# A four-layer graph network: step 1 of layer 3 propagates through half-size products, with sums of adj kept in DRAM

## The chip, the cores and the metric

The kernel runs on one core of a Trainium2 chip. A core has five engines that each take their own instructions in order: TensorE (PE, with its weight loads shown apart as PEld), VectorE (DVE), ScalarE (ACT), GpSimd (POOL) and SyncE (SP), which here only issues transfers. They wait for each other through semaphores. The metric is the device time of one execution in microseconds (us).

## The reference

The input is a node matrix x (3327 x 256) and one dense matrix adj (3327 x 3327) that all four layers share. Each layer normalises its input, takes the positive part and adds what the layer makes of it:

```python
h = relu(layernorm(x)); x = x + layer0(h, adj)     # adj @ (h W0' + b)
h = relu(layernorm(x)); x = x + layer1(h, adj)     # tanh(adj*adj), filtered, @ (tanh(h Wp + b) Wg), relu
h = relu(layernorm(x)); x = x + layer2(h, adj)     # D^-1/2 (adj+I) D^-1/2 @ (h W2'), relu
h = relu(layernorm(x)); x = x + layer3(h, adj)
# layer 3, on X = h:
R = adj + eye;  R = R / R.sum(-1, keepdims=True)
Xf = Xa = X;  Z = 0
for n in range(2):
    A  = top_p_attention(Xa)     # softmax((Xa W1'W2')(Xa W3')'), largest entries until 0.9, renormalised
    Xf = R @ Xf
    Xa = A @ Xa
    Z  = Z + Xf @ U1[n].T + Xa @ U2[n].T
out = layernorm(X + Z) * ln_g + ln_b
```

## The kernel before

The 3327 nodes are padded to T = 26 tiles of P = 128; H = 13 is half of them. adj comes transposed and cut into blocks: `adj_t[m, :, k, :]` is the block that carries tile k into tile m, and the diagonal of adj is full. All arithmetic is in fp32, and each fp32 product of two blocks shows in the profile as two matmul instructions.

**Layers 0 to 2** (`products`, L555) take row tiles in pairs, p and p + 13. A pair's four quadrants of adj (a11, a12, a22, a21, each 13 blocks) times the 2 x 2 quadrants of the right side (13 tiles deep, halves of 128 columns wide) are formed with 7 products in place of 8 (`Product`, L502): three of the left operands are quadrants (a11, a12, a22) and four are sums (s1 = a21 + a22, a21' = a11 − a21, s2 = s1 − a11, s4 = a12 − s2); the sums on the right are made once per layer. `Feed` (L451) loads the quadrants in three cuts of 5, 4 and 4 blocks through the SP queue, up to two cuts ahead (`load`), and VectorE makes the sums one cut ahead (`add`, L485–488). These matmuls are 128 columns wide (L520).

**Layer 3** (`layer_3_in`, L841) has two steps. Each has 26 rows of tiles, and for each row:

- attention: logits of one row tile (L914), their exponentials on ScalarE (L935), a search for the smallest kept entry (`search_steps`), a pass that zeroes the others (L1013), then the row turned block by block (L178, copied by ScalarE at L181) and multiplied with the node values (L189; `Rows.begin` and `Rows.finish`);
- propagation: R times the node tiles (`propagated_steps`, L1058): 26 matmuls of 128 x 128 by 128 x 256, with adj's row tile loaded as two slabs of 13 blocks (832 KB) from a pool of three buffers; GpSimd adds the identity to the diagonal block (L1068).

In step 1 the propagated tile is scaled by the inverse row sum on ScalarE (`xf`, L1110), turned (L138) and multiplied with U1 (`sums`, L1122), which writes `fs`, the operand of step 2's propagation. `AttentionOfFirstStep` scales attention's result by 1/den (`xa`, L1080), turns it, makes the keys of step 2 (`node`) and, with U2, `vs` and `z` (L1099, L1100; z goes to DRAM).

The search of one row starts with the row's sum (`total`, L952), a mean and a spread of the logits from it, and the first bound t: Ln, Ln and Exp on ScalarE (L953–955), `t = 2 mean − c` on VectorE (L956), Exp on ScalarE (L957). Two passes of ScalarE over the row follow (L968, L973), then VectorE's: one pass with the next bound (L984), extraction of candidates in four parts (L993, L997), five rounds of eight largest (L1002, L1005), and L1013.

**Order.** In layer 3 the instructions of TensorE stand in the order of the program (`manual_schedule` with PE alone); the hooks in `plan` (a dictionary from the number of a matmul to functions) interleave the rest with the matmuls of a row. The other engines' order is chosen by a planner, pushed by `high_priority` and `issue_after`. The first EARLY = 4 propagated tiles come ahead of the first attention row; LATE = 4 come at the end of step 1. Attention runs AHEAD = 3 rows ahead of its use. The rows in APART = (3, 7, 11, 15, 19) carry no propagation: they start the next logits and go on to the next row. Between the steps stands a branch on flags (L1254) behind which lies a fallback for searches that failed (`if_failed`).

Of the kernel before, what the change touches and what calls it, by code (L numbers as in the profile page):

```python
# [45 lines left out]
def kernel(  # L46
# [54 lines left out]
    hT_dram = dram.tile([P, T, NC, P], F32, name="hT_dram")  # L101

# [162 lines left out]
    def layers_0_to_2(again):  # L265
# [120 lines left out]
        class Pair:  # L386


            def __init__(self, layer, p, rhs, x2):
                self.layer, self.p, self.rhs = layer, p, rhs  # L390
                self.pool = work, "xT", 2
                self.name = f"{tag}{layer}_{p}"
                if layer == 3:
                    self.xn = pair_of(rhs.rows, p)
                    normed(self.name, x2, self.xn)
                    nc.vector.tensor_scalar(self.xn, self.xn, 0.0, None, ALU.max)
# [46 lines left out]
            def keys(self):  # L443
                for i in range(2):
                    m = self.p + i * H
                    add_nodes(kT0, ksum0, self.xT[:, :, i * P : (i + 1) * P], m, f"{self.name}_{i}", bank)
# [4 lines left out]
        class Feed:  # L451
# [3 lines left out]
            def __init__(self, layer, order, load_x, change=None, count=None):  # L455
                self.layer, self.order, self.load_x = layer, order, load_x
                self.change, self.count = change, count
                self.quads, self.ready, self.x2, self.done = {}, {}, {}, [0, 0]
# [17 lines left out]
            def add(self, p, c):  # L476
# [11 lines left out]
                nc.vector.tensor_tensor(s4, a12, s2, ALU.subtract)  # L488
                self.ready[p, c] = a11, a12, s4, a22, s1, s2, a21
# [115 lines left out]

        IN_ORDER = [(p, c) for p in range(H) for c in range(len(CUTS))]
# [56 lines left out]
        if not again:  # L663
# [31 lines left out]
            feed = Feed(0, order + IN_ORDER[2 * len(CUTS) :], load_x, count=count0)  # L695
# [67 lines left out]
        else:  # L763
# [57 lines left out]
            2, P, rhs2, Feed(2, IN_ORDER, from_rows(x2_dram), count=count2), finish2(rhs2), left,  # L821
# [19 lines left out]
    def layer_3_in(tag, big, ep, w3, sm3, h3, kT0, ksum0, left, at_end):  # L841


        fs = new_nodes(f"fs{tag}")[:, :, :D]
# [21 lines left out]
        gs = big.tile([P, D], F32, name="gs")  # L866
        nc.scalar.dma_start(gs, ln_g.partition_broadcast(P))
        bs = big.tile([P, D], F32, name="bs")
        nc.scalar.dma_start(bs, ln_b.partition_broadcast(P))
# [69 lines left out]
        def search_steps(step, m, e, parts, st, dens, alone):  # L939
# [12 lines left out]
            nc.vector.tensor_reduce(total, parts, AX.X, ALU.add)  # L952
# [3 lines left out]
            nc.vector.scalar_tensor_tensor(t, mean, 2.0, c, ALU.mult, ALU.subtract)  # L956
            nc.scalar.activation(t, t, AF.Exp)  # L957
# [70 lines left out]
        def failed(step, st):  # L1028
# [14 lines left out]
            pf = ps_acc.tile([P, 512], F32, tag="acc", name=f"pf_{step}")  # L1043
# [14 lines left out]
        def propagated_steps(acc, step, m, xf):  # L1058
# [3 lines left out]
            for n, k in enumerate(order):  # L1062
# [7 lines left out]
                yield n  # L1070

# [31 lines left out]
        class PropagationOfFirstStep:  # L1103


            def __init__(self, m, acc):
                self.m = m
                self.xf = w3.tile([P, D], F32, tag="xf", name=f"xf_{m}")
                with tc.high_priority():
                    nc.scalar.activation(self.xf, acc[:, :D], AF.Copy, scale=rinv[:, m : m + 1])  # L1110
                self.hT = w3.tile([P, NC, P], F32, tag="hT", name=f"hT_{m}")
                nc.sync.dma_start(self.hT, hT_dram[:, m])

# [4 lines left out]
            def sums(self):  # L1118
                acc = one_bank(f"u1_{self.m}")
                parts = [(xT[:, c, :], u1s[:, s, c, :]) for s, xT in enumerate((self.hT, self.xT)) for c in range(NC)]  # L1120
                for i, (xT, u) in enumerate(parts):
                    nc.tensor.matmul(acc[:, :D], xT, u, start=(i == 0), stop=(i == len(parts) - 1))  # L1122
                with tc.high_priority():
                    nc.scalar.copy(fs[:, self.m, :], acc[:, :D])

        def finish3(m, y, acc, name):
# [4 lines left out]
            x3 = w3.tile([P, D], F32, tag="xf", name=f"x3_{name}")  # L1131
# [49 lines left out]

        def keep_of_equal(e, t, target, s, name):
# [3 lines left out]
            rank, eq = (  # L1186
                slabs.tile([P, H, P], F32, tag="slab", name=f"{k}_{name}").rearrange("p k m -> p (k m)")
                for k in ("rank", "eq")
            )
            rank, eq = rank.bitcast(I16), eq.bitcast(U8)[:, :NP]  # L1190
# [88 lines left out]
        with tc.manual_schedule(engines=PE_ALONE):  # L1279
# [23 lines left out]
            def passes_apart(step, finder, late=False):  # L1303

# [5 lines left out]
                def more_of_first():  # L1310
                    with tc.high_priority(), tc.issue_after(last_turned[-1].ins):
                        next(finder)
# [257 lines left out]
```

## Time and profile before

| what | value |
|---|---|
| median of three runs | 2642.61 us (2639.8 to 2642.98) |
| the profiled execution | 2643.87 us |
| its span in the profile | 2641.7 us |
| PE busy | 2564.9 us (97%) |
| DVE busy | 2035.0 us (77%) |
| ACT busy | 1034.2 us (39%) |
| POOL busy | 284.2 us (11%) |
| step 1 of layer 3, from the first attention row (1028.4 to 1834.5 us) | 806.1 us |
| moved by DMA | 273.43 MB, mean 104 GB/s |

The span runs from the first to the last instruction in the profile; the execution has some 2 us around it. A row of the groups reads: line, engine, operation, output from inputs, shape, count, then busy us in all and mean ns of one, then the idle time before it and what ended most of it. In the waits view a row names the engine and line that waited, what for, the us in all, how many times, and the longest. In the timeline a row has its start, its length, engine, line, operation and count, and in brackets the idle time before it. DMA shares are of the core's 16 DMA engines.

### The profile page before, as it was taken

The page shows a single profiled execution, that of the slowest core. Times are in us where ns is not written, and L with a number is a line of the kernel's source. Part 1 is how long each engine was busy: PE and PEld are TensorE (multiplying, and loading weights), DVE is VectorE, ACT ScalarE, POOL GpSimd, SP SyncE. Part 2 cuts the span into 40 slices and gives each one's busy share as a digit, 9 for nine tenths or more (in the row PEclk, how much of TensorE's full clock was granted, in tenths as well). Part 3 has the DMA queues.
Part 4 walks back from the last instruction along what each step waited for, and adds up shares of the span by engine and source line. Part 5 has one row for each costly group of instructions (what it writes and reads, how often), then busy time and mean ns, then how long its engine had stood idle before and what let it go on. Part 6 is the DMA issues. An engine that isn't in the chain of part 4 may idle for free. (4 is left out here: it accounts for less than half of the span.)

```text
span 2641.7 us, 42749 instructions
## 1 busy us (share of the span) xinstructions
PE 2564.9 (97%) x15979; PEld 2213.1 (84%) x15979; DVE 2035.0 (77%) x5495; ACT 1034.2 (39%) x1873; POOL 284.2 (11%) x435
## 2 busy tenths in 40 slices
PE   6999999999999999999999999999999999999997
PEld 6999999999999987777777777787787888888786
DVE  6667689888877848787878778783888888888883
ACT  2110124343011115555555555553545454545541
POOL 2000010000000000000000000000032222223221
PEclk9999999999999999999999999999999999999999
DMA  6455546555566632111111111111221122122211
GB/s 221 139 165 168 155 146 191 168 163 175 178 198 197 198 110 85 61 36 61 59 61 35 60 36 61 34 61 66 79 75 66 64 90 70 64 70 84 70 65 52
DMA packets 141358, 273.43 MB, mean 104 GB/s; under 512 B 15427, under 2 KB 67904, under 8 KB 141120
## 3 DMA queue, kind: packets, MB, share of 16 engines
q1 hardware_dynamic: 115648, 252.49, 30.2%
q10 hardware_dynamic: 25472, 17.92, 2.2%
q8 instruction: 131, 2.15, 0.3%
q14 instruction: 107, 0.88, 0.1%
HBM read 248.20 MB, written 20.45 MB: 102 GB/s over the span
## 5 line engine op out<-in xcount | busy, mean ns | idle before, releaser
L181 ACT COPY eT_a<-pt_a 128x512 f32<-128x512 f32 (+1 forms) x364 | 196.1, 554 | 340.4 <-PE pt_a L178 340.2
L1069 PE MATMUL f<-h3a,slab3a 128*128 128x256 f32 x1352 | 324.3, 383 | 4.9 <-ACTq L1254 4.8
L189 PE MATMUL a<-h3a,eT_a 128*128 128x256 f32 x1352 | 321.5, 379 | 0.7 <-ACT eT_a L181 0.7
L189 PE MATMUL a<-vs,eT_a 128*128 128x256 f32 x1352 | 320.2, 381 | 0.2 <-ACT eT_a L181 0.2
L1069 PE MATMUL f<-fsa,slab3a 128*128 128x256 f32 x1352 | 312.7, 382 | 0.0
L1069 PEld LDWEIGHTS f<-h3a,slab3a 128*128 128x128 f32 x1352 | 246.6, 189 | 65.7 <-issue 28.9
L1069 PEld LDWEIGHTS f<-fsa,slab3a 128*128 128x128 f32 x1352 | 249.8, 189 | 52.7 <-issue 17.4
L997 DVE MAX8 cand_a<-w 128x8 f32<-128x128 f32 x1352 | 284.6, 279 | 3.9
L189 PEld LDWEIGHTS a<-h3a,eT_a 128*128 128x128 f32 x1352 | 245.7, 189 | 36.5 <-issue 6.7
L189 PEld LDWEIGHTS a<-vs,eT_a 128*128 128x128 f32 x1352 | 246.4, 190 | 31.7 <-ACT eT_a L181 0.7
L520 PE MATMUL acc_a<-tsa,s_a 128*128 128x128 f32 (+1 forms) x2028 | 268.5, 275 | 0.7 <-DVE tsa L332 0.7
L520 PE MATMUL acc_a<-tsa,a_a 128*128 128x128 f32 x2028 | 251.0, 275 | 2.0 <-DVE tsa L335 2.0
L520 PE MATMUL acc_a<-rhs,a_a 128*128 128x128 f32 (+1 forms) x2028 | 250.4, 276 | 0.0
L520 PEld LDWEIGHTS acc_a<-tsa,s_a 128*128 128x128 f32 x2028 | 247.4, 192 | 1.4 <-DVE tsa L332 1.1
L520 PEld LDWEIGHTS acc_a<-tsa,a_a 128*128 128x128 f32 x2028 | 239.6, 192 | 3.5 <-DVE tsa L335 2.6
L520 PEld LDWEIGHTS acc_a<-rhs,a_a 128*128 128x128 f32 x2028 | 238.4, 192 | 1.9 <-ACT rhs L412 0.4
L993 DVE SCALAR_TENSOR_TENSOR w<-e_a,t_a 128x896 f32<-128x896 f32 x208 | 224.8, 1081 | 3.9
L935 ACT ACTIVATE e_a<-pl_a 128x1024 f32<-128x1024 f32 x208 | 177.8, 860 | 113.5 <-PE pl_a L914 112.4
L178 PE MATMUL pt_a<-ident,e_a 128*128 128x128 f32 x1352 | 199.6, 273 | 1.9
L178 PEld LDWEIGHTS pt_a<-ident,e_a 128*128 128x128 f32 x1352 | 165.2, 141 | 39.5 <-ACT eT_a L181 9.5
L984 DVE SCALAR_TENSOR_TENSOR w<-e_a,t_a 128x3328 uint8<-128x3328 f32 x52 | 191.6, 3685 | 3.6
L1013 DVE SCALAR_TENSOR_TENSOR e_a<-e_a,all_least 128x3328 f32<-128x3328 f32 x52 | 191.6, 3685 | 1.9
(208 smaller groups left out, 3366.1 us busy)
## 6 DMA issues: line engine op xcount, KB each, us to landing
slab3a<-in_adj_t_dram SPq DMA_DIRECT2D x104, 832.0 KB, 6.0
a_a<-in_adj_t_dram SPq DMA_DIRECT2D x312, 256.0 KB, 3.4
a_a<-in_adj_t_dram SPq DMA_DIRECT2D x156, 320.0 KB, 3.4
x_dram<-x_a ACTq DMA_DIRECT2D x39, 256.0 KB, 3.2
x_a<-x_dram SPq DMA_DIRECT2D x26, 256.0 KB, 3.2
hT_dram<-xT_a ACTq DMA_DIRECT2D x26, 128.0 KB, 3.5
hT<-hT_dram SPq DMA_DIRECT2D x26, 128.0 KB, 2.0
z_dram<-z SPq DMA_DIRECT2D x26, 128.0 KB, 1.7
```

Of the source, the lines that this page charges most:

```text
L178: nc.tensor.transpose(pt[:, j, :], e[:, k * P : (k + 1) * P], ident)
L181: last_turned.append(nc.scalar.copy(eT[:, : len(blocks), :], pt[:, : len(blocks), :]))
L189: nc.tensor.matmul(acc[:, :width], ready[g][:, j, :], rhs[:, k, :], start=(k == 0), stop=(k == T - 1))
L520: nc.tensor.matmul(self.acc[:, g, at : at + wide], quads[n][:, k - CUTS[c][0], :], t, start=(k == 0 and n in (1, 4)), stop=(k == H - 1 and ...
L935: last_exp.append(nc.scalar.activation(dst, src, AF.Exp, accum_out=parts[:, c : c + 1]))
L984: nc.vector.scalar_tensor_tensor(junk, e, t, e, ALU.is_lt, ALU.mult, accum_out=got)
L993: nc.vector.scalar_tensor_tensor(w[:, : (b - a) * P], eg, t, eg, ALU.is_lt, ALU.mult, accum_out=below[:, g : g + 1])
L997: nc.vector.max(cand[:, 8 * k : 8 * k + 8], w[:, (k - a) * P : (k - a + 1) * P])
L1013: nc.vector.scalar_tensor_tensor(e, e, least, e, ALU.is_ge, ALU.mult, accum_out=st["kept"][:, m : m + 1])
L1069: nc.tensor.matmul(acc[:, :D], slab[g][:, j, :], xf[:, k, :], start=(n == 0), stop=(n == T - 1))
```

## The change

1. In step 1 of layer 3 the propagation of a pair of row tiles is made with 7 half-size products (`FirstStepsPair`), 13 blocks deep and 128 columns wide, in two phases: products 1, 2, 5, 4 (52 matmuls), then 7, 3, 6 (39); for the first pair 1, 2, 3, then 5, 4, 7, 6. A phase stands where one row tile's 26 matmuls stood. Each product has one slab of 13 blocks. ScalarE copies the first accumulator (`half`), VectorE forms the four results with five instructions (`whole`), and `scale` multiplies with the inverse row sums on ScalarE.
2. The sums on the right, of h3's halves, are made at the start of layer 3 (`combine_h3`) and take the buffer that held `fs`. `sums` now writes its result to DRAM through SP (rows 12 and 25 of `fs` directly), and `fs` is loaded into h3's buffer on ScalarE's queue at the start of step 2.
3. The sums on the left come from DRAM: layer 0 writes them for pairs 2, 4, ..., 12 and layer 2 for pairs 0, 1, 3, ..., 11 (`KEPT`), four transfers for each cut of a kept pair, on SP's queue (`Feed.add`).
4. In the search ScalarE makes `total` (with an accumulating copy) and t (with −c as the bias of an Exp); VectorE has no part in them.
5. The row after an APART row no longer has its passes later than other rows (`late`). One propagated tile moves from the next-to-last row to the one before it. In rows, the turn of a propagated tile comes two groups later, with its scaling ahead of it. gs and bs take the place of u1s and are loaded in step 2. The fallback's spare tiles come from elsewhere.

```diff
@@ Feed.add @@
                 nc.vector.tensor_tensor(s4, a12, s2, ALU.subtract)
+                if p in self.keep:
+                    for n, s in enumerate((s1, s2, a21, s4)):
+                        nc.sync.dma_start(s_dram[:, p, n, a:b, :], s)
                 self.ready[p, c] = a11, a12, s4, a22, s1, s2, a21
@@ products @@
+        KEPT = range(2, H, 2), [0, *range(1, H, 2)]
@@ layer_3_in @@
-            fs = new_nodes(f"fs{tag}")[:, :, :D]
+        ts = new_nodes(f"ts3{tag}").rearrange("p t d -> p (t d)")[:, : 4 * H * P]
+        ts = ts.rearrange("p (n k f) -> p n k f", n=4, k=H)
...
@@ search_steps @@
-            nc.vector.tensor_reduce(total, parts, AX.X, ALU.add)
+            nc.scalar.activation(parts, parts, AF.Copy, accum_out=total)
             nc.scalar.activation(mean, total, AF.Ln, scale=1.0 / N)
             nc.scalar.activation(lnv, mean, AF.Ln, bias=tiny, scale=2.0)
             nc.scalar.activation(c, lnv, AF.Exp, bias=ln_z, scale=0.5)
-            nc.vector.scalar_tensor_tensor(t, mean, 2.0, c, ALU.mult, ALU.subtract)
-            nc.scalar.activation(t, t, AF.Exp)
+            nc.scalar.activation(lnv, c, AF.Copy, scale=-1.0)
+            nc.scalar.activation(t, mean, AF.Exp, bias=lnv, scale=2.0)
@@ new in layer_3_in @@
+        PHASES = (1, 2, 5, 4), (7, 3, 6)
+        FIRST_PHASES = (1, 2, 3), (5, 4, 7, 6)
+        PLACE3 = {2: (0, 0), 1: (0, 1), 4: (0, 2), 5: (0, 3), 6: (1, 0), 7: (1, 1), 3: (1, 2)}
+
+        def combine_h3(a, b):
+            def part(i, j):
+                return h3[:, i * H + a : i * H + b, j * P : (j + 1) * P]
+
+            t1, t2, t3, t4 = (ts[:, n, a:b, :] for n in range(4))
+            nc.vector.tensor_tensor(t1, part(0, 1), part(0, 0), ALU.subtract)
+            nc.vector.tensor_tensor(t2, part(1, 1), t1, ALU.subtract)
+            nc.vector.tensor_tensor(t4, part(1, 0), t2, ALU.subtract)
+            nc.vector.tensor_tensor(t3, part(1, 1), part(0, 1), ALU.subtract)
+
+        class FirstStepsPair:
...
+            def load(self, n):
+                p = self.p
+                x = self.slabs[n] = slabs.tile([P, H, P], F32, tag="slab", name=f"slab3{tag}_0_{p}_{n}")
+                if n in (1, 2, 4):
+                    i, j = {1: (0, 0), 2: (0, 1), 4: (1, 1)}[n]
+                    nc.sync.dma_start(x, adj_t[p + i * H, :, j * H : (j + 1) * H, :])
+                else:
+                    nc.sync.dma_start(x, s_dram[:, p, {5: 0, 6: 1, 7: 2, 3: 3}[n]])
+                if n in (1, 4, 5, 7):
+                    nc.gpsimd.tensor_tensor(x[:, p, :], x[:, p, :], ident, ALU.add)
...
+            def steps(self, phase):
...
+                    if n not in self.slabs:
+                        self.load(n)
...
+                    nc.tensor.matmul(
+                        self.accs[bank][:, c * P : (c + 1) * P], a, self.right(n, k),
+                        start=start, stop=last.get(bank) == (n, k), skip_group_check=True,
+                    )
+                    yield at
+
+            def half(self):
+                self.y = w3.tile([P, 4, P], F32, tag="xf", name=f"xf_{self.name}")
+                with tc.high_priority():
+                    nc.scalar.copy(self.y.rearrange("p n f -> p (n f)"), self.accs[0])
+
+            def whole(self):
+                y, b = self.y, self.accs[1].rearrange("p (n f) -> p n f", f=P)
...
+                with tc.high_priority():
+                    nc.vector.tensor_tensor(y[:, 0, :], y[:, 0, :], y[:, 1, :], ALU.add)
+                    nc.vector.tensor_tensor(y[:, 1, :], y[:, 1, :], b[:, 0, :], ALU.add)
+                    nc.vector.tensor_tensor(y[:, 2:4, :], y[:, 2:4, :], both(y[:, 1:2, :]), ALU.add)
+                    nc.vector.tensor_tensor(y[:, 1, :], y[:, 3, :], b[:, 2, :], ALU.add)
+                    nc.vector.tensor_tensor(y[:, 2:4, :], y[:, 2:4, :], both(b[:, 1:2, :]), ALU.add)
@@ PropagationOfFirstStep @@
-                with tc.high_priority():
-                    nc.scalar.activation(self.xf, acc[:, :D], AF.Copy, scale=rinv[:, m : m + 1])
+            def scale(self, behind=last_turned):
+                with tc.issue_after(behind[-1].ins):
+                    nc.scalar.activation(self.xf, self.xf, AF.Copy, scale=rinv[:, self.m : self.m + 1])
...
-                    nc.scalar.copy(fs[:, self.m, :], acc[:, :D])
+                    nc.scalar.copy(rows, acc[:, :D])
+                if not last:
+                    nc.sync.dma_start(fs_dram[:, self.m, :], rows)
@@ the rows of step 1 @@
+            with tc.issue_after(left.made.ins):
+                combine_h3(0, H - 1)
+            combine_h3(H - 1, H)
             for i in range(EARLY):
...
-                    plan = {5: [p.turn], 16: [p.sums]}
+                    plan = {6: [lambda: p.scale(last_exp)], 13: [p.turn], 20: [p.sums]}
...
-                plan, later = passes_apart(0, finder, m - 1 in APART) if interleaved else (passes(finder), {})
+                plan, later = passes_apart(0, finder) if interleaved else (passes(finder), {})
...
-                    plan = merged(plan, {1: [p.turn], 5: [p.sums]})
+                    plan = merged(plan, {2 if interleaved else 1: [p.scale], 3: [p.turn], 5: [p.sums]})
@@ the start of step 2 @@
+            fs.append(new_nodes(f"fs{tag}")[:, :, :D])
+            for k in range(0, T, H):
+                for a, b in ((k, k + 6), (k + 6, k + H - 1)):
+                    nc.scalar.dma_start(fs[0][:, a:b, :], fs_dram[:, a:b, :])
+            rows_of_first(H - 1)
```

## The prediction

> **What bounds the kernel now.** I read the page's busy shares first, then a table of engines by stage, the waits of TensorE, and the timeline around the longest of them. The page says TensorE: 97% of the span.
>
> ```profile
> PE 2564.9 (97%) x15979; PEld 2213.1 (84%) x15979; DVE 2035.0 (77%) x5495; ACT 1034.2 (39%) x1873; POOL 284.2 (11%) x435
> ...
> L1069 PE MATMUL f<-h3a,slab3a 128*128 128x256 f32 x1352 | 324.3, 383 | 4.9 <-ACTq L1254 4.8
> ...
> slab3a<-in_adj_t_dram SPq DMA_DIRECT2D x104, 832.0 KB, 6.0
> a_a<-in_adj_t_dram SPq DMA_DIRECT2D x312, 256.0 KB, 3.4
> ```
>
> The L1069 group is what the change replaces: 26 tiles of 26 blocks, two instructions for each fp32 product, 1352. By stage (span, then PE busy, then DMA share and GB/s at the end): the body of step 1 of layer 3, one pair of tiles in layer 2, and a short stretch of that layer.
>
> ```profile
> 1028.40:1834.50 806.10, 787.46 (x3917) 616.73 (x3915) 593.76 (x1791) 420.18 (x781) 13.43 (x66) 1.00 0.15 52
> 801.96:823.72 21.76, 21.76 (x197) 21.75 (x196) 17.19 (x39) 2.35 (x8) 1.28 (x2) 1.00 0.64 184
> 822.50:825.00 2.50, 2.50 (x25) 2.50 (x24) 1.04 (x3) 0.60 (x1) 0.00 (x0) 1.00 0.94 318
> ```
>
> In layer 2 TensorE never rests. In step 1 it rests 18.6 of 806.1 us, with DVE (third column of pairs) at 74%. The waits view says on what:
>
> ```profile
> PE pt_a L138 <- ACT xa L1080: 6.8, 5, 1.4
> PE pl_a L914 <- DVE z L1100: 6.2, 5, 1.3
> PE f L1069 <- ACTq L1254: 4.8, 1, 4.8
> PE pt_f L138 <- ACT xf L1110: 4.1, 3, 2.9
> ```
>
> The first two belong together, five times each, after the five rows (3, 7, 11, 15, 19) that carry no propagation. One of the five, from the timeline:
>
> ```profile
> 1165.60 3.69 DVE L1013 SCALAR_TENSOR_TENSOR e_a<-e_a,all_least 128x3328 f32<-128x3328 f32 x1
> ...
> 1169.69 1.13 PE L914 MATMUL pl_a<-kT_0a,qT 64*128 64x512 f32 x4 [1.23 <-DVE z L1100]
> 1169.80 0.20 ACT L957 ACTIVATE t_a<-t_a 128x1 f32<-128x1 f32 x1 [4.20 <-DVE t_a L956]
> 1170.09 3.07 ACT L968 ACTIVATE junk_a<-e_a,t_a 128x3328 uint8<-128x3328 f32 x1
> ...
> 1173.66 0.44 PE L138 MATMUL pt_a<-ident,xa 128*128 128x128 f32 x2 [1.35 <-ACT xa L1080]
> ```
>
> DVE's full-row pass of the row that ends (3.69 us) holds up the small op L956 of the next search; ScalarE waits for it 4.2 us, in order, then does a 3.07 us pass, and xa, which TensorE needs, comes behind. The stretches 1150–1200 and 1250–1300 have 46.86 and 46.87 us of busy PE in 50: about 3.1 us lost each, of which the two waits name 2.6. Five of them: 15.6 us. So two things set the end of step 1: the number and width of TensorE's instructions, and these five stops.
>
> **The products.** What does a 128-wide instruction cost against a 256-wide one? The means of one (383, 275 ns) overlap their neighbours, so I take starts:
>
> ```profile
> 1116.66 2.75 PE L1069 MATMUL f<-h3a,slab3a 128*128 128x256 f32 x12
> 1119.26 0.60 PE L242 MATMUL pkq<-xT_a,kq 128*128 128x128 f32 x4
> ...
> 806.86 2.40 PE L520 MATMUL acc_a<-rhs,a_a 128*128 128x128 f32 x20
> 809.10 1.28 PE L520 MATMUL acc_a<-tsa,s_a 128*128 128x128 f32 x10
> ```
>
> Twelve 256-wide ones take 1116.66 to 1119.26, 0.217 each; twenty 128-wide ones 806.86 to 809.10, 0.112 each. A row's seven propagation groups, first start of each to the next group's start (0.52, 1.40, 2.60, 1.39, 2.70, 0.86, 2.16 us), sum to 11.63 us for 52 instructions; 26 rows: 302.4. After, a pair has 7 products of 13 blocks of 2 instructions, 182 x 0.112 = 20.4 us, plus the same excess for changes of group (11.63 − 52 x 0.2164 = 0.38 a phase, 0.76 a pair): 13 x 21.14 = 274.9. **−27.5 us.** By busy sums it would be −25 (L1069's 324.3 against 2366 x 0.1265, the mean share of L520's three groups, 769.9 us for 6084); exactly an eighth, −38. I take the starts.
>
> Here a rule speaks against the change. The Trainium skill ("TensorE: Matmul & The Clock Gate", Back-to-back issue gap) gives a stream of weight loads and matmuls about 81 ns at 128 columns and 131 at 512, since the weight load counts too; between them, 256 columns would be some 98 (my estimate, on a line). By that ratio 7/8 as many products at half width, thus 7/4 as many instructions, would cost 302 x 1.75 x 81/98 = 437 us: 135 slower. The rows, in this kernel and fp32, say 0.112 to 0.217, a ratio of 0.52, in the same order weight load, matmul. The rows decide.
>
> **ScalarE makes the first bound.** total, the negated exponent and t move from DVE to ScalarE, so the 4.2 us wait goes, and L968's 3.07 us start with it; xa is then ready before TensorE asks. z still stands behind the full-row pass only if that pass does. Per row ScalarE gets two small ops of about 0.3 us more; it is 52% busy. But DVE's order of the changed kernel has the next row's first extraction op (L993's kind, 3.69 us for four) ahead of the final pass of rows 8, 16 and 24. Rows 8 and 16 follow a row that carries only the short phase of a pair (39 products, 37.0 us of row): e is ready about 37.7 after the row's start (7.3 to the first extraction, 24.5 of search by the row at 1120.32–1144.83, the inverted 3.7, 1.4 of pair sums, small ops), and TensorE wants it at 34.5. These two keep a stop of about 3 us; rows 4, 12, 20 lose theirs. **−9.3** (−15.6 to 0).
>
> **First results.** xf at 1016.28 (the 2.9 us wait) is now scaled and turned seven units apart: **−2.9**.
>
> **Entry.** Four DVE ops of 128x1536 make the sums of h3 as step 1 starts. L487 at 512 takes 0.69 us, at 640 0.82, so 1.75 each, 7 us, at 968–975 where PE waits 2.3 us already; mean keys and the last node tile stand in the same queue. **+1.5** (−1 to +5).
>
> **Slabs in the early rows.** A slab of 13 blocks now serves 13 narrow products, 26 x 0.112 = 2.9 us (4.2 with the work between), where it served 5.8. It takes 4.8 us (single) to 6.0 (median) from issue to landing, plus 0.46 of POOL for four slabs in seven. Three buffers leave two slabs' use, 6 to 8.4 us, for 5.5 needed. **+3** with the scattered tails (0 to +7). In the steady rows other work doubles the cover.
>
> **The writes in layers 0 and 2.** Thirteen pairs (six in layer 0, seven in layer 2) each send 12 transfers, 3.41 MB, down SP's queue, between the loads of the next quarters; each write waits for its DVE sum, and the loads queued behind wait with it. In 697–959.5 that queue moved 41.17 MB for 53.2% of the DMA engines' time: 295 GB/s at full use. A kept pair thus adds 11.6 us of DMA to a pair of 21.76 that uses 0.64 to 0.72: 1.17 to 1.25, some 4 to 5.5 us late; in layer 0 (0.54 in 60–340) 1.08. The next pair, not kept, has 6 to 8 spare; only pairs 0 and 1 of layer 2 are both kept, 9 late. Sums are made early: s1 by DVE at 804.19, read by TensorE at 816.47, 12 us. The lateness fits in there. A second rule to weigh: the skill ("DMA: Bandwidth & Descriptors", Where 436 GB/s comes from) sets about 358 GB/s of HBM per core; 210 + 157 = 367 at most and 341 for the pair shown would be just at that, and cost nothing; by the rows (318 GB/s at 0.94 share) it doesn't fit and eats slack. **+2** by the rows (0 to +25), 0 by the rule.
>
> **At no cost.** ScalarE's copy of 128x512 (0.55 by L181's row) and DVE's five ops a pair lie under interleaved attention (TensorE waits only if DVE's 79% becomes a bound: a rival). Writing fs and reloading it in four transfers of 768 KB: 11 to 18 us by the slabs' 6.0 each and their overlap, against 20 us of row 0's own work in step 2; without that cover up to 15. The branch's 4.8 stays. Step 2 is PE-bound at 29.0 us a row whatever ScalarE does.
>
> **Sum.** −27.5 − 9.3 − 2.9 + 1.5 + 3 + 2 = −33.2 against the profiled 2643.9 (2641.7 of span and 2.2 around it): 2610.7; the median of the runs is 1.3 lower: **2609 us**.
>
> **Rivals.**
> - *All five stops go* (e is never late): 6 more, and slabs fit: 2600. For it: the same 16 us (e at 1111.3, used at 1127.6). Against: the order of rows 8 and 16.
> - *Search becomes the bound of step 1*: rows of 30.6 us instead of 33.5 with 24 us of DVE leave it tight; e comes late after all five rows and often else: the stops stay (2618), and 7 us go in other rows: 2625. For it: DVE at 74%, by the shorter rows at 79%. Against: 16 us between e and its use in ordinary rows.
> - *The writes saturate DMA*: each of 13 pairs stops TensorE. Break-even at 33/13 = 2.6 us a pair, which needs lateness of 12 + 2.6 us, or the same from loads standing behind waiting writes on SP; at 4 us a pair: 2609 + 52 = 2661 at worst, **slower**; half of that leaves 2635. Against: that needs twice the DMA share worked out. For: SP's order, and peaks of 0.92–0.98 already.
> - *Narrow products gain nothing*, the rule above: weight loads of 190 ns a mean bind: 2637 (the other terms make −5.7), slower if the ratio is over 0.58. Against: layer 2's cadence.
>
> **Chances.** My forecast (2602–2618) 0.55; all stops go 0.13; search binds 0.17; writes 0.11 (0.05 of it slower); narrow products 0.04 (0.02 slower). A difference below 0.2%, 5.3 us, can't be told from none. Faster 0.90, same 0.03, slower 0.07. The range to 8 in 10: 2596 (all stops go, and entry and writes cost nothing) to 2633 (writes at half their worst, nearly).
>
> **What would show it.** Right: TensorE's group for step 1's products has 2366 instructions; its body is 30 us shorter; no ScalarE wait on t; stops of 3 us only before rows 8 and 16; layers 0 and 2 end at the same times within 3 us with DMA shares near 1 in kept pairs. Wrong: TensorE waiting on s or a tiles in layers 0 and 2 (writes), on the slabs or POOL early in layer 3 (buffers), on DVE's e in rows past 4 (search), or products starting more than 0.115 us apart.

## The result, and the profile after

The changed kernel takes 2629.78 us (median of 6 runs, 2624.72 to 2633.79); before, on the same chips, 2642.07 us (6 runs). The ratio is 0.9953, 95% interval 0.994 to 0.9966: 12.4 us faster, where 33 were forecast. The profiled execution took 2624.72 us, its span 2622.9; it was the quickest of the six, so the times by stage below lean to the good side.

The page of the changed kernel, its rows for what was shown of before:

```profile
PE 2539.9 (97%) x16993; PEld 2238.4 (85%) x16993; DVE 2058.3 (78%) x5464; ACT 1076.4 (41%) x2042; POOL 330.5 (13%) x461
...
a_a<-in_adj_t_dram SPq DMA_DIRECT2D x312, 256.0 KB, 3.9
slab3a<-in_adj_t_dram SPq DMA_DIRECT2D x91, 832.0 KB, 4.7
...
slab3a<-s_dram SPq DMA_DIRECT2D x52, 832.0 KB, 4.5
s_dram<-s_a SPq DMA_DIRECT2D x78, 256.0 KB, 3.1
```

The group of step 1's products, from the groups of TensorE:

```profile
L1140 PE MATMUL f_a<-ts3a,slab3a 128*128 128x128 f32 x1352 | 169.9, 276 | 0.6 <-DVE ts3a L1090 0.6
L1140 PE MATMUL f_a<-h3a,slab3a 128*128 128x128 f32 x1008 | 132.6, 280 | 3.2 <-ACT lnv_a L963 3.1
L1140 PE MATMUL f_a<-h3a,ends 128*128 128x128 f32 x6 | 1.0, 275 | 0.0
```

They are 2366 instructions, as counted in advance. The first thing to read is where the stages stand. These are the groups of instructions with which the propagation of step 1 and of step 2 begins, before and after; a row has their count, shortest, median and longest time in ns, then the start of the first and of the last:

```profile
L1069 PE MATMUL f<-h3a,slab3a x1352: 377/379/793, 959.6 to 1877.2; 128*128 128x256 f32 x194
L1069 PE MATMUL f<-fsa,slab3a x1352: 377/378/484, 1894.9 to 2624.9; 128*128 128x256 f32 x194
```

```profile
L1140 PE MATMUL f_a<-h3a,slab3a x1008: 270/275/580, 977.5 to 1853.0; 128*128 128x128 f32 x168
L1078 PE MATMUL f<-fsa,slab3a x1352: 377/378/484, 1876.4 to 2606.3; 128*128 128x256 f32 x194
```

TensorE's first instruction of step 1's propagation starts at 959.59 us before and at 977.46 after; its first of step 2's propagation at 1894.91 and 1876.37; the rest of the span is 746.8 and 746.6. So:

| stage | before, us | after, us | difference | forecast |
|---|---|---|---|---|
| layers 0 to 2 | 959.6 | 977.5 | +17.9 | +2 |
| layer 3, up to step 2's propagation | 935.3 | 898.9 | −36.4 | −35.2 |
| step 2 | 746.8 | 746.6 | −0.2 | 0 |

Layer 3 did what was forecast. Half of its gain was lost in the layers that the change only asks to write something down. The loss is not spread over them. Layer 2's first product starts at 674.46 us before and at 677.47 after, layer 1's at 371.13 and 372.64: so layer 0, with six kept pairs, lost 1.5 us, as much as layer 1, which keeps none, and layer 2, with seven, lost 14.9. In 40 to 340 us the DMA share rose from 0.54 to 0.68, and TensorE was busy 297.0 us before and 296.0 after. In the two runs below that take the writes away or add them alone the loss lies in layer 2 as well (15.9 and 15.5 us).

The waits of TensorE in layer 2 (697 to 960 us) of the changed kernel:

```profile
PE pt_a L373 <- DVE h3a L400: 8.9, 5, 2.1
PE acc_a L527 <- DVE tsa L335: 1.0, 1, 1.0
```

and before:

```profile
PE acc_a L520 <- DVE tsa L335: 0.2, 1, 0.2
```

h3a are the node tiles of layer 3 that VectorE makes from a pair's result; TensorE turns them in the next pair, at a fixed place, and five times they are not there. One of the five in the timeline, with what VectorE did ahead of it:

```profile
757.90 0.69 DVE L629 SCALAR_TENSOR_TENSOR pos<-a_a,pos 128x512 bf16<-128x512 f32 x1 [3.16 <-DMA a_a<-in_adj_t_dram]
...
762.45 0.68 DVE L665 TENSOR_TENSOR x_a<-x_a,y_a 128x512 f32<-128x512 f32 x1
...
767.15 0.82 DVE L629 SCALAR_TENSOR_TENSOR pos<-a_a,pos 128x640 bf16<-128x640 f32 x1
767.88 0.42 DVE L400 TENSOR_SCALAR h3a<-h3a 128x512 f32<-128x512 f32 x1
...
768.36 0.66 PE L373 MATMUL pt_a<-ident,h3a 128*128 128x128 f32 x4 [1.95 <-DVE h3a L400]
```

and the same pair before:

```profile
753.44 0.42 DVE L396 TENSOR_SCALAR h3a<-h3a 128x512 f32<-128x512 f32 x1
753.78 0.82 DVE L621 SCALAR_TENSOR_TENSOR pos<-a_a,pos 128x640 bf16<-128x640 f32 x1
...
758.43 0.60 PE L370 MATMUL pt_a<-ident,h3a 128*128 128x128 f32 x4
```

VectorE counts the entries of each quadrant (L629) soon after its load, waits there 3.16 us for the load to land, and the pair's result, its normalisation and h3a stand behind it. Before, h3a was ready at 753.86 and used at 758.43: a slack of 4.6 us, less than half of the 12 us that I took from the sums.

The wait is only a part of it. From the end of the pair's last product to h3a there were 12.1 us before (741.74 to 753.86): VectorE worked 10.2 of them and stood idle 2.0. After, there are 18.75 us (749.55 to 768.30), 13.6 of work and 5.1 idle. VectorE is further behind TensorE, so work that it had done by the pair's end now comes after it.

Its order is another one, too. In the rows above, the counting of the next 640-wide block (L629, L621) stands ahead of h3a after the change and behind it before. The planner sets this order when the kernel is built. In the changed kernel, and in tiny_writes and before_with_writes below, one more counting pass stands ahead of h3a in every second pair of layer 2, and one less in the others. Without the writes VectorE's order in layer 2 is that of before; with them on GpSimd's or ScalarE's queue it is so in nearly every pair. So the writes on SP act in two ways: through the queues, and through the order that the planner gives VectorE.

### The profile page after: what moved, and what is told of

Read it like the earlier page. It is cut to its first block, busy times and chain, and to the rows that moved or that the text cites. A ratio compares the mean times of both kernels' runs of the same rounds, so it can differ in the third digit from the quotient of the medians.

```text
span 2622.9 us, 45628 instructions
## 1 busy us (share of the span) xinstructions
PE 2539.9 (97%) x16993; PEld 2238.4 (85%) x16993; DVE 2058.3 (78%) x5464; ACT 1076.4 (41%) x2042; POOL 330.5 (13%) x461
## 5 line engine op out<-in xcount | busy, mean ns | idle before, releaser
L993 DVE SCALAR_TENSOR_TENSOR w<-e_a,t_a 128x3328 uint8<-128x3328 f32 x52 | 191.6, 3684 | 4.0 <-DVE t_a L990 0.9
L376 ACT ACTIVATE xT_a<-pt_a 128x512 f32<-128x512 f32 x52 | 30.8, 593 | 361.3 <-PE pt_a L373 340.5
L1140 PEld LDWEIGHTS f_a<-ts3a,slab3a 128*128 128x128 f32 x1352 | 161.5, 192 | 20.3 <-issue 18.5
```

Source lines behind the costliest of these rows:

```text
L376: nc.scalar.activation(dst.rearrange("p f n -> p (f n)"), pt.rearrange("p f n -> p (f n)"), func)
L993: nc.vector.scalar_tensor_tensor(junk, e, t, e, ALU.is_lt, ALU.mult, accum_out=got)
L1140: nc.tensor.matmul(self.accs[bank][:, c * P : (c + 1) * P], a, self.right(n, k), start=start, stop=last.get(bank) == (n, k), skip_group_ch ...
```

## The experiments

Differences are worked out from the ratios to the kernel before (times 2642 us), since the chips differ by some 2 us; "against the change" is the ratio less 0.9953. Two intervals taken together leave most of these differences uncertain by some 5.6 us (my estimate: the root of the summed squares of their half-widths, 0.0017 and 0.0013). So −3.2, −5.0 and +5.5 are not clear of nothing, and two differences of 7 and 8 us can't be told apart. The last column is one profiled execution of each: where TensorE's first instruction of step 1's propagation starts. Layers 0 to 2 are the same program in the change, bound_by_dve and rows_in_order, and there it varies by 3.6 us. no_writes and tiny_writes load other blocks in place of the sums, so their step 1 works on other numbers.

| run | median, us | ratio, 95% interval | against the change, us | layer 3 begins, us |
|---|---|---|---|---|
| the change | 2629.8 | 0.9953, 0.994 to 0.9966 | | 977.5 |
| no_writes | 2604.7 | 0.9864, 0.9847 to 0.988 | −23.5 | 955.2 |
| before_with_writes | 2665.1 | 1.009, 1.0073 to 1.0107 | (before: +23.8) | 978.1 |
| tiny_writes | 2612.4 | 0.9895, 0.9878 to 0.9911 | −15.3 | 966.5 |
| spread_writes | 2631.1 | 0.9956, 0.9942 to 0.997 | +0.8 | 983.0 |
| spread_hooks | 2625.8 | 0.9941, 0.9924 to 0.9958 | −3.2 | 977.6 |
| writes_on_act | 2636.6 | 0.9974, 0.9957 to 0.999 | +5.5 | 984.7 |
| writes_on_pool | 2622.9 | 0.9921, 0.9905 to 0.9938 | −8.5 | 977.4 |
| hooks_later | 2621.9 | 0.9927, 0.991 to 0.9943 | −6.9 | 977.4 |
| pool_and_hooks | 2611.9 | 0.989, 0.9874 to 0.9907 | −16.6 | 968.1 |
| count_later | 2624.6 | 0.9934, 0.9917 to 0.995 | −5.0 | 976.4 |
| deeper_loads | 2644.3 | 1.0013, 1.0006 to 1.0019 | +15.9 | 997.4 |
| cuts_of_four | 2642.5 | 1.001, 1.0 to 1.0019 | +15.1 | 992.3 |
| deeper_pool_hooks | 2633.9 | 0.9975, 0.9967 to 0.9983 | +5.8 | 983.0 |
| bound_by_dve | 2642.6 | 1.0005, 0.9998 to 1.0011 | +13.7 | 976.3 |
| rows_in_order | 2619.6 | 0.9907, 0.9891 to 0.9924 | −12.2 | 979.9 |
| three_cures | 2608.3 | 0.9866, 0.985 to 0.9883 | −23.0 | 968.5 |

### Is it the writes?

```diff
 # no_writes: Feed.add, then the loads of the slabs
-                if p in self.keep:
-                    for n, s in enumerate((s1, s2, a21, s4)):
-                        nc.sync.dma_start(s_dram[:, p, n, a:b, :], s)
...
-                    nc.sync.dma_start(x, s_dram[:, p, {5: 0, 6: 1, 7: 2, 3: 3}[n]])
+                    nc.sync.dma_start(x, adj_t[p + H, :, :H, :])
...
 # before_with_writes: the same three lines added to the kernel before, with KEPT
```

> The changed kernel without the writes of the sums in layers 0 and 2; the slabs that held the sums are loaded from a quadrant of adj instead (same size, so step 1's propagated tiles are not the reference's; the attention and its searches don't read them in step 1). Theory W (the writes alone took the missing part): layer 3 begins near 960 us as before, and the whole takes 2643.9 - 36.4 = 2607 to 2611 us. Rival O (the rest of the change moved the order of layers 0 to 2 or slowed their entry into layer 3): layer 3 still begins 5 to 18 us late, 2617 to 2630 us.

> The kernel before with only the writes of the sums added, on SP's queue and for the same pairs; nothing reads them. Theory W: layers 0 to 2 take 18 us more, 2660 us. If the writes cost what I forecast, 2644 to 2646 us.

Without the writes layer 3 begins at 955.25 us and the kernel takes 23.5 us less than the changed one; with them alone the kernel before takes 23.8 us more. The two agree: the writes cost 24 us in either kernel, and without them the change would bring 36 us (forecast, with 2 for the writes, 33). Nothing else in layers 0 to 2 is seen to cost anything: without the writes layer 3 begins 4.3 us earlier than before the change. From here on the question is how writes whose results nothing waits for cost 24 us.

### Overload in the pairs that are kept?

The forecast had counted 4 to 5.5 us of overload in each kept pair. The pairs of layer 2 in the changed kernel, by windows from one copy of results to the next (DMA share and GB/s at the end of a row), kept and not kept by turns:

```profile
751.61:774.02 22.41, 20.46 (x184) 20.26 (x183) 16.39 (x38) 2.34 (x9) 1.15 (x2) 1.00 0.96 311
774.02:798.24 24.22, 24.22 (x220) 24.21 (x219) 18.24 (x41) 2.34 (x9) 1.28 (x2) 1.00 0.67 216
798.24:819.40 21.16, 19.52 (x176) 19.32 (x175) 16.46 (x38) 2.34 (x9) 1.25 (x2) 1.00 0.96 319
819.40:841.56 22.16, 22.16 (x201) 22.15 (x200) 17.74 (x40) 2.34 (x9) 1.28 (x2) 1.00 0.66 214
```

That looked like the answer, so I spread the same bytes over all pairs.

```diff
-                if p in self.keep:
-                    for n, s in enumerate((s1, s2, a21, s4)):
-                        nc.sync.dma_start(s_dram[:, p, n, a:b, :], s)
+                for n, s in enumerate((s1, s2, a21, s4)):
+                    if n in self.keep.get(p, ()):
+                        nc.sync.dma_start(s_dram[:, p, n, a:b, :], s)
-        KEPT = range(2, H, 2), [0, *range(1, H, 2)]
+        KEPT = {p: (0, 1) for p in range(2, H)}, {p: (0, 1, 2, 3) if p < 2 else (2, 3) for p in range(H)}
 # spread_hooks: also WHERE_KEYS = (84, 90)
```

> The changed kernel with the same 44 MB of writes spread out: layer 0 writes two of the four sums of every pair from 2 on, layer 2 the other two (all four for pairs 0 and 1). A pair of layer 2 then wants 0.64 + 0.27 = 0.91 of the DMA engines instead of 1.17 in one pair and 0.64 in the next. Theory P (only the overload in kept pairs costs): nearly all of the 25 us that the writes cost comes back, 2605 to 2612 us. Rival Q (each write costs, whatever the load of its pair: its place in SP's queue, its hold on a tile): 2624 to 2631 us.

> Spread writes as in the run beside it and the later transposes of hooks_later. Theory P: with no lateness left the later place gains nothing more, 2604 to 2612 us. Rival Q: 2617 to 2623 us, the 8 us of the later place alone.

The load is even now, and nothing came back. Windows of 22 us in layer 2, and the waits of TensorE there:

```profile
774.00:796.00 22.00, 22.00 (x199) 21.99 (x199) 17.31 (x40) 2.34 (x8) 1.08 (x2) 1.00 0.81 260
796.00:818.00 22.00, 22.00 (x199) 21.99 (x199) 16.94 (x39) 2.56 (x9) 1.08 (x2) 1.00 0.84 271
```

```profile
PE pt_a L373 <- DVE h3a L400: 9.8, 5, 3.0
PE acc_a L527 <- DVE tsa L335: 3.1, 1, 3.1
```

Theory P falls: in 730 to 862 us no window of 22 us is above 0.89 of the DMA engines, and the same tile comes late, for as long. Two things are left that this run does not rule out: shorter bursts at full share, and VectorE's order, which is another one again here.

### The order on SP, or the bytes?

```diff
 # tiny_writes (the slabs loaded from adj as in no_writes)
-                        nc.sync.dma_start(s_dram[:, p, n, a:b, :], s)
+                        nc.sync.dma_start(s_dram[:, p, n, a : a + 1, :], s[:, :1, :])
 # writes_on_act, writes_on_pool
-                        nc.sync.dma_start(s_dram[:, p, n, a:b, :], s)
+                        nc.scalar.dma_start(s_dram[:, p, n, a:b, :], s)     # or nc.gpsimd
```

> The changed kernel with the same 156 writes at the same places of SP's queue and behind the same sums, but each of one block of its four or five (a quarter to a fifth of the bytes); the slabs come from adj, so step 1's propagated tiles are not the reference's. Theory S (the writes' place in SP's order and their waits make the loads late): as slow as the changed kernel, 2624 to 2630 us. Theory Y (the bytes make the loads' landings later): near the kernel without writes, 2605 to 2610 us.

> The changed kernel with the same writes issued on ScalarE's queue and not on SP's. Theory S (loads stand behind writes on SP that wait for VectorE's sums): layer 3 begins near 962 us, 2612 us. Theory B (bandwidth: the same bytes in the same pairs): 2628 to 2632 us; ScalarE's own copies then wait behind the writes, which could make it slower still, 2640 us.

> The changed kernel with the writes on GpSimd's queue. GpSimd has two small operations for each pair in layer 2. Theory S (it is the order on SP): 2610 to 2616 us. Theory P (the bytes in a kept pair): 2624 to 2632 us; GpSimd's own operation, which the node tiles need, then stands behind writes that wait for VectorE, so up to 2645 us.

Neither theory alone. The same queue entries with about a quarter of the bytes cost 8.2 us (0.9895 less 0.9864), the rest of the bytes another 15.3, with nearly the same order of VectorE in both kernels. Full writes on GpSimd's queue cost 15.1 us (0.9921 less 0.9864), with VectorE's order of before. So most of the cost goes with the bytes, in either order. What the other 8 us are is not parted: the places in SP's queue, the small writes' own bytes, or VectorE's order, which changes together with the place on SP. (In the profiled execution of writes_on_pool, the slowest of four, layer 3 begins where it does in the changed kernel, so its gain is seen in the medians alone.) On ScalarE's queue the waits for h3a are gone, but ScalarE's own copies stand behind the writes, and TensorE waits for its xT tiles instead (4.3 us at 794, 3.7 at 937): no better than on SP.

How long a 256 KB load takes from issue to landing in 700 to 955 us (the median, at the end of a row), before, in the changed kernel and in pool_and_hooks of the next section:

```profile
a_a<-in_adj_t_dram SPq DMA_DIRECT2D x88, 256.0 KB, 3.4
```

```profile
a_a<-in_adj_t_dram SPq DMA_DIRECT2D x91, 256.0 KB, 5.1
```

```profile
a_a<-in_adj_t_dram SPq DMA_DIRECT2D x92, 256.0 KB, 5.5
```

It is 3.6 us without writes, 3.9 with tiny, 4.6 with spread writes: at a mean share of 0.82 landing is slower than before the change at 0.63. But it does not set the cost by itself. With the writes on GpSimd's queue it is 5.4, and 5.5 in pool_and_hooks, whose layer 2 is nearly clean: both are quicker kernels than the changed one, with slower landings. When a load is issued may count as much; these medians don't show it.

### Is it VectorE's order that hands the lateness on?

```diff
 # hooks_later (pool_and_hooks: and the writes on GpSimd's queue)
-        WHERE_KEYS = (74, 89)
+        WHERE_KEYS = (84, 90)
 # count_later: Feed.load, Feed.add
                     q[i, j] = s
-                if self.count:
-                    self.count(p, c, q)
...
                 q = self.quads.pop((p, c))
+                if self.count:
+                    self.count(p, c, q)
```

> The changed kernel with the transposes of a pair's new node tiles ten products later (at 84 instead of 74 of 91) and the keys at 90 instead of 89, in layer 2 alone. Theory V (VectorE, in order, waits for late loads in its counting pass, so the node tiles come about 2 us after TensorE asks; nothing else of layer 2 is late): the five waits of 2 us go, 2629.8 - 10 = 2620 us. Rival B (the DMA engines are full, lateness only moves to the next thing that TensorE needs): 2627 to 2630 us, with TensorE waiting for sums or later tiles.

> The changed kernel with the writes on GpSimd's queue and the transposes of layer 2 ten products later. The queue gave 6.9 us alone, the later place 7.9. If they cure different waits, 2629.8 - 14.8 = 2615 us; if both cure the same five waits for node tiles, 2621 us.

> The changed kernel with the counting passes of VectorE one cut later, where the sums of the same cut are made, so that they don't wait for a load that has just been issued. Theory V (lateness reaches TensorE because VectorE, in order, waits for fresh loads in its counting pass with the pair's results behind it): VectorE's waits of 54 us for loads in layer 2 nearly go, TensorE's waits for h3 tiles, counts and sums too, 2606 to 2612 us. Rival: loads themselves come too late for TensorE's products, or the sums wait in the passes' place: 2622 to 2630 us.

In part. Turning the tiles 2.2 us later in the pair clears the waits for h3a. By the medians that gives 6.9 us; in the profiled execution layer 3 begins at 977.4 us all the same, and the edit has changed VectorE's order too (the same number of counting passes ahead of h3a in each pair). TensorE's waits in 697 to 960 us fall from 10.1 to 5.8 us, so some lateness moves on to the sums of layer 2's products, and rival B is right in part:

```profile
PE acc_a L527 <- DVE tsa L335: 3.2, 1, 3.2
PE acc_a L527 <- DVE s_a L492: 2.2, 2, 1.3
PE pkq_a L245 <- DVE counts L640: 0.4, 2, 0.2
```

With the writes on GpSimd's queue as well the two gains add by the medians (8.5 and 6.9 alone, 16.6 together). Here the profile agrees: layer 3 begins 9.4 us earlier than in the changed kernel, and layer 2 is nearly clean:

```profile
PE pkq_a L245 <- DVE counts L640: 1.0, 5, 0.2
PE acc_a L527 <- DVE tsa L335: 0.7, 1, 0.7
PE acc_a L527 <- DVE tsa L338: 0.2, 1, 0.2
PE acc_a L527 <- DVE s_a L492: 0.2, 1, 0.2
```

Of the writes' 24 us some 7 are left (0.989 less 0.9864). Counting later was meant to free VectorE from waiting for fresh loads. It did not do that: its wait for loads in 697 to 960 us stayed at 53.4 us (53.2 in the changed kernel), since the sums of the same cut want the same loads. It brought 5 us by the medians, which is not clear of nothing, and tells only that the place of the counting alone is not the way.

### Are loads late for want of buffers?

```diff
-CUTS = ((0, 5), (5, 9), (9, 13))
+CUTS = ((0, 4), (4, 7), (7, 10), (10, 13))
-                    s = raw.tile([P, 5, P], F32, tag=f"a{i}{j}", name=f"a{i}{j}_{name}")[:, : b - a, :]
+                    s = raw.tile([P, 4, P], F32, tag=f"a{i}{j}", name=f"a{i}{j}_{name}", bufs=4)[:, : b - a, :]
-                for k, (ahead, what) in enumerate(((2, self.load), (1, self.add))):
+                for k, (ahead, what) in enumerate(((3, self.load), (1, self.add))):
 # cuts_of_four: the new CUTS and tile sizes alone
```

> The changed kernel with cuts of 4, 3, 3 and 3 blocks in place of 5, 4 and 4, four buffers for each quadrant in place of three, and loads one cut further ahead. Theory J (the loads are issued only when TensorE frees a buffer and land just in time, so every us that writes add to their landing is a us of VectorE, whose slack is 4 us): a load then has a cut more to land, and the 25 us mostly come back, 2606 to 2613 us. Rival F (the DMA engines are too full whatever the buffers): 2622 to 2630 us.

> The same cuts of 4, 3, 3 and 3 blocks with three buffers and loads two cuts ahead as before: the control for the run beside it. Loads are smaller and VectorE has a third more instructions on them, while less is loaded ahead: theory J 2630 to 2645 us; rival F the same time as the deeper loads, within 3 us.

> All three: deeper loads, writes on GpSimd's queue, transposes later. Theory J with the rest of the waits gone: 2604 to 2609 us, as without writes. Rival F: 2613 to 2620 us.

The smaller cuts cost 15 us by themselves, and the fourth buffer changed nothing on top. But VectorE's wait for loads in 697 to 960 us was again 53.0 us with it (44.1 in cuts_of_four), so the loads were no earlier for it, and theory J is not tested by this pair of runs: it is neither shown nor refuted. On top of pool_and_hooks the deeper loads cost 22 us (0.9975 less 0.989): 2633.9 us, where 2604 to 2609 were expected under theory J and 2613 to 2620 under rival F.

### Layer 3: the first bound, and the order of the rows

```diff
 # bound_by_dve: total and t as before the change
 # rows_in_order, in search_steps
-            nc.vector.scalar_tensor_tensor(junk, e, t, e, ALU.is_lt, ALU.mult, accum_out=got)
+            with tc.issue_after(last_kept[-1].ins) if step == 0 and last_kept else nullcontext():
+                nc.vector.scalar_tensor_tensor(junk, e, t, e, ALU.is_lt, ALU.mult, accum_out=got)
...
-            nc.vector.scalar_tensor_tensor(
+            last_kept.append(nc.vector.scalar_tensor_tensor(
                 e, e, least, e, ALU.is_ge, ALU.mult, accum_out=st["kept"][:, m : m + 1]
-            )
+            ))
```

> The changed kernel with the first bound made as before, by ScalarE and VectorE in turn. My forecast put the move to ScalarE at 9.3 us: 2629.8 + 9.3 = 2639 us, with ScalarE waiting 4 us for t after rows 3, 7, 11, 15 and 19. If the move did nothing because other waits take its place: 2630 us; if all five stops come back on top of those before rows 8 and 16: 2645 us.

> The changed kernel with one edit in step 1's searches: a row's full pass with its second bound (3.69 us) is held until the row before it has had its final pass. My forecast said that this inversion keeps a stop of about 3 us before rows 8 and 16; the trace of the changed kernel shows stops of 2.4 and 2.0 there and 2.0 before row 0. If the inversion is the cause these go: 2629.8 - 6 = 2623 us, or 2620 if the TensorE clock then drops less often. If VectorE is simply short of time in these rows, the stop moves to the next row: 2629 us.

> Writes on GpSimd's queue, transposes of layer 2 ten products later, and step 1's final passes in order: 2611.9 - 6 = 2606 us if they add up, 2611 us if the last gives nothing.

With VectorE in the first bound again, three stops of 2.7 us come back in rows 4, 12 and 20 (at 1168, 1411.6 and 1654.9 us), those that the forecast said would go. The first of them:

```profile
1167.99 2.50 PE L192 MATMUL a<-h3a,eT_a 128*128 128x256 f32 x5 [2.66 <-ACT eT_a L184]
```

The time rises by 13.7 us (9.3 forecast), a little more than the whole change had won, and in the profile step 1 takes 912.2 us instead of 898.9. Three stops are 8 us of that; the clock, which fell after two of them (below), is another 3.4. The stops that the forecast said would stay are in the changed kernel's timeline; this is the one before row 8:

```profile
1272.41 3.69 DVE L993 SCALAR_TENSOR_TENSOR w<-e_a,t_a 128x3328 uint8<-128x3328 f32 x1
1276.03 3.68 DVE L1022 SCALAR_TENSOR_TENSOR e_a<-e_a,all_least 128x3328 f32<-128x3328 f32 x1
...
1279.77 0.44 PE L181 MATMUL pt_a<-ident,e_a 128*128 128x128 f32 x2 [2.42 <-DVE e_a L1022]
```

L993 is the next row's pass and stands ahead of this row's last one. In rows_in_order they have changed places:

```profile
1273.72 3.68 DVE L1025 SCALAR_TENSOR_TENSOR e_a<-e_a,all_least 128x3328 f32<-128x3328 f32 x1
1277.33 3.68 DVE L996 SCALAR_TENSOR_TENSOR w<-e_a,t_a 128x3328 uint8<-128x3328 f32 x1
```

All three stops of this kind are gone and no other came. By the medians that is 12.2 us, but with the uncertainty above, and the profile shows less: step 1 takes 893.1 us, 5.8 less, about their 6.4 us of waiting. three_cures gives the same answer against pool_and_hooks: 6.3 us by the medians, and step 1 of 891.5 us after 898.1. So the order of the rows is worth some 6 us, as expected, and the other 6 of the 12.2 are not shown to come from it. three_cures takes 2608.3 us, 0.9866 of before, the quickest version here with all its work done and as quick as the changed kernel without the writes (0.9864).

## Why the prediction was wrong

The step that failed is "The writes in layers 0 and 2", at +2 us with a bound of +25. It measured +17.9 in the profiled execution and 24 by the runs that take the writes away or add them. The sign that was named for it did not show either: TensorE never waited for an s or an a tile in the changed kernel, and layer 3 still began late. The range given, 2596 to 2633, holds 2629.8 because its upper end allowed for writes at half their worst; the forecast of 2609 had no place for them.

- **Its mechanism.** It said "The lateness fits in there", in the 12 us between making and reading a sum. That is the wrong reader. The sums weren't late first; the pair's node tiles were, with 4.6 us of slack, because VectorE works in order and waits for loads ahead of them, and because the planner put more of its work ahead of them in every second pair. How much each does is open. I had a row for the first (VectorE waited 66.9 us for loads in its counting pass already before the change) and gave it no term.
- **Its size.** It counted DMA time above 100%. Spread evenly, at 0.8 to 0.9, the same bytes cost as much, and 8 of the 24 us come without most of the bytes. The two rules for bandwidth that I weighed answered a question that didn't decide; and the 358 GB/s of the second is no ceiling here, since with the writes on GpSimd's queue one stretch of 6.4 us in layer 2 moved 413 GB/s. Nor is it the same cost for each pair: the 1.08 worked out for layer 0 cost 1.5 us there at most, the 1.17 to 1.25 in layer 2 nearly all of it. Why is not tested.
- **The rival** with the writes had the place right and the mechanism wrong: it needed lateness of 12 + 2.6 us a pair, where 4.6 us were enough to be late. Its second way, loads standing behind writes on SP, can be a part of the 8 us that come without most of the bytes.
- **The clock.** Two stops in layers 0 to 2 were followed by a drop of the clock (below), 1.7 us each, and one before (at 38.80 us). So 1.7 of the 17.9 us are the clock, which no term had.

The other terms, against the profile of the changed kernel:

- Products, −27.5: from each start to the next with idle time taken out, one of the 256-wide ones took 0.224 us in the rows before (303 for 1352), and one narrow one 0.1156 (195.6 us for 1692 in 1066–1783), 273.5 for 2366: about −29.5. The ratio of 81 to 98 that the prediction drew from the skill's page does not hold for these fp32 streams; it is 0.516. (The sign "more than 0.115 us apart" was set too close to the 0.112 of the forecast.)
- First bound, −9.3: 13.7 by its run. The stops stayed where it said (2.4 and 2.0 us) and nearly went where it said: in rows 4, 12 and 20 TensorE still waits about 1 us each for z (3.1 in all). The inverted op was wrongly named: it is the next row's pass with its second bound (L984 before the change), not its extraction; length and place were right.
- First results, −2.9: the wait is gone. A wait of 1.1 us for xf at 1869 stands where there were two of 0.6 before.
- Entry, +1.5: TensorE waits 2.8 us there, before 2.0 (the prediction has 2.3): +0.8.
- Early slabs, +3: no wait for a slab anywhere in the waits of TensorE. A wait of 2.0 us for row 0's e, by the same inversion, stood there instead.
- "The branch's 4.8 stays": 3.1 us for ScalarE and 3.5 for VectorE's first small ops of step 2's search came in its place, +1.8, and the clock stayed low 3.4 us longer there.
- The reload of fs: no wait for it, as said.

That layer 3's sum came out within 1.2 us is in part luck: the products and the first bound brought more than their terms, the slabs' 3 us never came, and stops and the branch took some back.

## What to carry to other kernels

A transfer that nothing waits for is not free where loads arrive just as an in-order engine asks for them: price it by the slack of everything queued behind that wait, not only by the slack of the data it carries or by the bandwidth left. An engine's waits for loads cost nothing only as long as something else ends later; before adding traffic, find the first tile behind them that the bounding engine needs and its slack. Where a planner orders the engines, compare its order before and after as well: an edit of the queue can move other work. When such a term is large and cheap to take away, measure it alone: one run without the writes told what they cost, if not how.

## What the runs showed of the hardware

TensorE's granted clock can halve for 3.4 us just after a stop, in these profiles after stops of 1.4 to 2.6 us. Around the stop of 2.60 us at 318.31 in the changed kernel (the column before the last two is the clock):

```profile
315.90:319.30 3.40, 0.99 (x5) 0.92 (x6) 3.32 (x6) 0.00 (x0) 0.00 (x0) 1.00 0.45 140
319.40:322.80 3.40, 3.40 (x15) 3.05 (x14) 2.70 (x7) 0.58 (x1) 0.00 (x0) 0.50 0.00 0
322.90:326.30 3.40, 3.40 (x33) 3.40 (x32) 2.10 (x7) 0.48 (x1) 0.00 (x0) 1.00 0.30 81
```

and before, where the stop at the same place is 1.76 us:

```profile
319.50:322.90 3.40, 3.40 (x29) 3.30 (x28) 2.96 (x8) 0.80 (x2) 0.00 (x0) 1.00 0.28 69
```

In 3.4 us TensorE does 15 instructions in place of 29, so such a stop costs 1.7 us more than it lasts. The same happens after 2.08 us of waiting at 690.66. It is not a plain threshold. The stop before row 8 has no such drop in the changed kernel, where it lasts 2.42 us, and has one in pool_and_hooks, where it lasts 1.98. Before the change stops of 2.48 us (at 617.46) and 2.95 (at 1016.28) had none, and one of 1.43 at 38.60 was followed by 3.4 us at 0.50. The Trainium skill ("TensorE: Matmul & The Clock Gate", HAM oscillation — how this bites in real kernels) asks for no idle gaps over some 3.4 us; here shorter ones were enough. The same page (What's actually happening) has the clock set by a free-running window of that length. That may be why equal stops differ, as a window can hold one stop whole and cut another in two, but no run here tests it. What remains open is why a load lands later at 0.8 of the DMA engines, how many of the 15 us that the bytes cost go through VectorE's waits, and how many of the 24 through its order.
